# Attention probabilities turned by VectorE and DMA instead of TensorE, in a two-layer kernel in float32

## The chip, the cores and the metric

One core of a Trainium2 chip (trn2) runs the whole program. The metric is the device time of one execution in microseconds (us). Three runs of the kernel before took 1148.38, 1147.91 and 1146.68 us; the median is 1147.91 us. The profile is of one execution.

The engines are named as in the profile: PE is TensorE (PEld its weight loads), DVE is VectorE, ACT is ScalarE, POOL is GpSimd, SP is SyncE, whose queue issues nearly all DMAs here. SBUF and PSUM have 128 partitions; a "quarter" is 32 partitions that lie together.

## The reference, cut to what matters

The input x is 16 sequences of 256 tokens with 256 features, all in float32. Layer 0 is a normalisation, a linear recurrence and a gated feed-forward; the change does not touch it. Layer 1 is, with `S = 256`:

```
xn = layernorm(x)
q  = xn @ Wq                     # 16 heads, 128 plain + 64 rotary features
c, k_rope = split(xn @ Wkv_a)    # 64 latent + 64 rotary features, shared by all heads
k_nope, v = split(rmsnorm(c) @ Wkv_b)
scores = q . [k_nope, k_rope] / sqrt(192), masked so that a query sees keys up to itself
attn   = softmax(scores)
s      = (attn . v) @ Wo
x      = x + s * silu(base(x) + gated low-rank experts)
```

The kernel folds `Wkv_b` into the queries and into `Wo`. Each head then has queries of 128 features (64 latent, 64 rotary), all heads have the same keys `kT` (128 features) and the same 64 values per key (`row[:, :, 0:64]`), and attention returns 64 numbers per head and query.

## The kernel before

**Chunks and units.** The 4096 tokens are 8 chunks (`NCH`) of 512 (`CH`): two sequences, four blocks of 128 tokens. In layer 1 a chunk has 4 groups of 4 heads; a group has two units, one for each sequence (`b` = 0 and 1). So there are 64 units, 8 to a chunk, in the order chunk, group, sequence. A pair is the two units of one group.

**Scores of a unit** (`score_pack`, L644 to L675). The partitions hold 4 heads x 32 queries, so 8 query blocks `a` of 32 cover the sequence, and block `a` needs 32(a+1) keys. The blocks go in three packs, (7, 6), (5, 4, 3) and (2, 1, 0). For each pack PE writes `sc`, DVE adds the diagonal mask (L660) and takes the negative maximum `nm` (L662), ACT writes the exponentials to `pr` with their sum `sr` (L667), DVE inverts the sum (L672) and POOL scales `pr` (L675). Three `pr` buffers (`NPR = 3`) serve the units in turn.

**Turning the probabilities** (`turn_part`, L680 to L688). The value matmul needs keys on the partitions. For each unit PE transposes twelve 128x128 blocks of `pr` into the one buffer `pt` of PSUM, four blocks to a call, and ACT copies each 128x512 result to `pT`. The three calls of a unit stand in step i+2 of unit i (`LAG = 2`).

**Values of a unit** (`values`, L690 to L707): 8 matmuls of `pT` with `row` into `av`, then a DVE copy to `attT`. They stand in step i+3.

**Queries of the next group** (`query_tile`, L588 to L629), four tiles to a group, two in each step. Tiles 0 and 1 are the rotary part: DVE multiplies by the rotation (L610), POOL combines into `qrot` (L622, L623), and eight DMAs on SP's queue (L626) move quarters of `qrot` into partitions 64 to 127 of `qg`. Tiles 2 and 3 are the latent part, scaled by ACT into partitions 0 to 63 of `qg` (L616). Both go by PE (L606).

**Extras.** In each step one or two pieces of other work follow the packs: the preparation of the next chunk (`norm_chunk`, `transpose_chunk`, `kv_chunk`, `router_chunk`, `key_chunk`, `mid_chunk`, `gate_part`) and the output projection of the last one (`finish_part`, L709 to L721: 8 matmuls, a product on DVE, a sum on POOL, a DMA to HBM).

**Order.** The tile scheduler orders each engine's instructions from the program order and its own estimates. An engine then works its list strictly in that order. SP's queue, too, takes one DMA after the other, and a DMA whose data are not ready holds up those behind it.

Of the kernel before, what the change touches and what calls it, by code (L numbers as in the profile page):

```python
# [18 lines left out]
P = 128  # L19
B, S, D = 16, 256, 256  # L20
NTOK = B * S
CH = 512
# [17 lines left out]
@with_exitstack  # L40
def tile_two_layers(ctx: ExitStack, tc: tile.TileContext, d: dict, out: bass.AP):
    nc = tc.nc

    const = ctx.enter_context(tc.tile_pool(name="const", bufs=1))
    xpool = ctx.enter_context(tc.tile_pool(name="xres", bufs=1))
# [364 lines left out]
    pp = ctx.enter_context(tc.tile_pool(name="p1", bufs=2))  # L410
    fix = ctx.enter_context(tc.tile_pool(name="fix1", bufs=1))
    ps_sc = ctx.enter_context(tc.tile_pool(name="ps_sc", bufs=3, space=PSUM))
    ps_pt = ctx.enter_context(tc.tile_pool(name="ps_pt", bufs=1, space=PSUM))
    ps_m1 = ctx.enter_context(tc.tile_pool(name="ps_m1", bufs=4, space=PSUM))

    class Chunk:
        pass
# [14 lines left out]
    def kv_chunk(ch):  # L432

        k = chunks[ch]
        pkv = ps_m1.tile([P, TPC, P], F32, tag="m1", name=f"pkv_{ch}")
        for j in range(TPC):
            for c in range(2):
                nc.tensor.matmul(  # L438
                    pkv[:, j, :], k.xnT[:, c, j * P : (j + 1) * P], wkva[:, c, :],
                    start=(c == 0), stop=(c == 1),  # L440
                )
# [12 lines left out]
        ra = a2.tile([P, TPC, ROPE], F32, tag="ra", name=f"ra_{ch}", bufs=1)  # L454
        rb = a2.tile([P, TPC, ROPE], F32, tag="rb", name=f"rb_{ch}", bufs=1)
        nc.vector.tensor_tensor(ra[:, :, 0:HR], x1, rope_k[:, 0], ALU.mult)
        nc.vector.tensor_tensor(ra[:, :, HR:ROPE], x2, rope_k[:, 0], ALU.mult)
        nc.vector.tensor_tensor(rb[:, :, 0:HR], x2, rope_k[:, 1], ALU.mult)
        nc.vector.tensor_tensor(rb[:, :, HR:ROPE], x1, rope_k[:, 2], ALU.mult)
        nc.gpsimd.tensor_tensor(row[:, :, KVL:P], ra, rb, ALU.add)  # L460
        k.row = row

    def key_chunk(ch):
        k = chunks[ch]
        row = k.row
        pk = ps_m1.tile([P, CH], F32, tag="m1", name=f"pk_{ch}")
        for j in range(TPC):
            nc.tensor.transpose(pk[:, j * P : (j + 1) * P], row[:, j, :], ident)
        k.kT = a2.tile([P, CH], F32, tag="kT", name=f"kT_{ch}")
        nc.vector.tensor_copy(k.kT, pk)  # L470

    def router_chunk(ch):
# [4 lines left out]
        for jp in range(2):  # L477
            pm = ps_m1.tile([P, 2, 256], F32, tag="m1", name=f"pm_{ch}_{jp}")
            for j2 in range(2):
                j = 2 * jp + j2  # L480
                for c in range(2):
                    nc.tensor.matmul(  # L482
                        pm[:, j2, 0 : P + NE], k.xnT[:, c, j * P : (j + 1) * P], wmid[:, c, :],
                        start=(c == 0), stop=(c == 1),
                    )
# [46 lines left out]
    def mid_chunk(ch):  # L532
        k = chunks[ch]
        mg = k.mg
        pmT = ps_m1.tile([P, CH], F32, tag="m1", name=f"pmT_{ch}")
        for j in range(TPC):
            nc.tensor.transpose(pmT[:, j * P : (j + 1) * P], mg[:, j, :], ident)
        k.mT = a2.tile([P, CH], F32, tag="mT", name=f"mT_{ch}")
        nc.vector.tensor_copy(k.mT, pmT)

    def gate_part(ch, jp):
# [5 lines left out]
        for j2 in range(2):  # L547
            cols = slice((2 * jp + j2) * P, (2 * jp + j2 + 1) * P)
            for c in range(2):
                nc.tensor.matmul(  # L550
                    pg[:, j2, :], k.xnT[:, c, cols], wbase[:, c, :],
                    start=(c == 0), stop=False,
                )
            nc.tensor.matmul(pg[:, j2, :], k.mT[:, cols], wlb, start=False, stop=True)  # L554
# [17 lines left out]
    for h in range(G):  # L572
# [14 lines left out]
    def query_tile(ch, g, t):  # L587
# [3 lines left out]
        if t == 0:  # L591
            q = groups[ch, g] = Group()
            q.qg = qp.tile([P, CH // 32, G, 32], F32, tag="qg", name=f"qg_{n}")
            q.rot = qp.tile([P, 2, CH], F32, tag="qrot", name=f"qrot_{n}")
            q.mul = [
                qp.tile([P, 2, CH], F32, tag="qmul", name=f"qmul_{n}_{r}", bufs=3) for r in range(2)
            ]
        q = groups[ch, g]
        ps = ps_m1.tile([P, CH], F32, tag="m1", name=f"pq_{n}_{t}")
        for c in range(2):  # L600
            if t < 2:
                w = wrope[:, c, g, t, :, :].rearrange("p h f -> p (h f)")
            else:
                h0 = g * G + 2 * (t - 2)
                w = wlat[:, c, h0 : h0 + 2, :]
            nc.tensor.matmul(ps, w, k.xnT[:, c, :], start=(c == 0), stop=(c == 1))  # L606
        if t < 2:
            ps2 = ps.rearrange("p (b s) -> p b s", b=2)
            for r in range(2):
# [21 lines left out]
    class Unit:  # L631


        def __init__(self, i):
# [5 lines left out]
            self.nm = sm.tile([P, NQ], F32, tag="nm", name=f"nm_{self.n}")  # L640
            self.sr = sm.tile([P, NQ], F32, tag="sr", name=f"sr_{self.n}")

    def score_pack(u, pi):
        k, b, pack = chunks[u.ch], u.b, PACK[pi]  # L644
        qg = groups[u.ch, u.g].qg
        sc = ps_sc.tile([P, CH], F32, tag="sc", name=f"sc_{u.n}_{pi}")
        for a, o in pack:
            nc.tensor.matmul(  # L648
                sc[:, o : o + 32 * (a + 1)], qg[:, b * NQ + a, :, :].rearrange("p h q -> p (h q)"),
                k.kT[:, b * S : b * S + 32 * (a + 1)], start=True, stop=True,  # L650
            )
# [23 lines left out]
            nc.gpsimd.tensor_scalar(v, v, u.sr[:, a : a + 1], 1.0, ALU.mult, ALU.mult)  # L675


    BLOCKS = [(a, 0) for a in range(NQ)] + [(a, 1) for a in range(4, NQ)]

    def turn_part(u, z):  # L680
        if z == 2:
            u.pT = pp.tile([P, 12, P], F32, tag="pT", name=f"pT_{u.n}")
        pt = ps_pt.tile([P, CH], F32, tag="pt", name=f"pt_{u.n}_{z}")
        for y in range(4):
            a, kb = BLOCKS[4 * z + y]
            o = OFF[a] + kb * P
            nc.tensor.transpose(pt[:, y * P : (y + 1) * P], u.pr[:, o : o + P], ident)  # L687
        nc.scalar.copy(u.pT[:, 4 * z : 4 * z + 4, :], pt.rearrange("p (y f) -> p y f", y=4))  # L688

    def values(u):  # L690
        k, b = chunks[u.ch], u.b
        av = ps_m1.tile([P, 2, S], F32, tag="m1", name=f"av_{u.n}")
        for p2 in range(2):
            for kb in range(2):
                for hh in range(2):
                    hc = slice(32 * (2 * p2 + hh), 32 * (2 * p2 + hh) + 32)
                    nc.tensor.matmul(  # L697
                        av[64 * hh : 64 * hh + 64, p2, P * kb : S].rearrange(
                            "p (a q) -> p a q", q=32
                        ),  # L700
                        k.row[:, 2 * b + kb, 0:KVL],
                        u.pT[:, 8:12, hc] if kb else u.pT[:, 0:8, hc],
                        start=(kb == 0), stop=(kb == 1),
                    )
        if b == 0:
# [3 lines left out]
    def finish_part(ch, j):  # L709
        k = chunks[ch]  # L710
        po = ps_m1.tile([P, CH], F32, tag="m1", name=f"po_{ch}_{j}")
        for p in range(NPAIR):
            nc.tensor.matmul(  # L713
                po[:, 0:D], k.attT[p // 2][:, p % 2, j * P : (j + 1) * P], wout[:, p, :],
                start=(p == 0), stop=(p == NPAIR - 1),
            )
# [13 lines left out]
    router_chunk(0)  # L730
    key_chunk(0)
    mid_chunk(0)
    for jp in range(2):
        gate_part(0, jp)


    PER = 2 * NG
    LAG = 2
    LAST = NCH * PER
    units = {}  # L740
    turned = None
    for i in range(LAST + LAG + 1):
        ch, r = divmod(i, PER)

        extra = []
        if ch > 0 and LAG < r < LAG + 5:
            extra.append(lambda: finish_part(ch - 1, r - LAG - 1))
        if ch + 1 < NCH:
            extra += {
                0: [lambda: norm_chunk(ch + 1)],  # L750
# [5 lines left out]
                6: [lambda: gate_part(ch + 1, 0)],  # L756
                7: [lambda: gate_part(ch + 1, 1)],
            }[r]
        u = w = nq = None
        v = turned  # L760
        if i < LAST:
            u = units[i] = Unit(i)
            nxt = i // 2 + 1
            if nxt < LAST // 2:
                nq = (*divmod(nxt, NG), 2 * (i % 2))
        if LAG <= i < LAST + LAG:
            w = units.pop(i - LAG)
        extra += [None] * (2 - len(extra))
        for z in range(3):
            if u:  # L770
                score_pack(u, z)
            if v and z == 0:
                values(v)
            if w:
                turn_part(w, 2 - z)
            if z < 2:
                if nq:
                    query_tile(nq[0], nq[1], nq[2] + z)
                if extra[z]:
                    extra[z]()  # L780
        turned = w
    for j in range(TPC):
        finish_part(NCH - 1, j)


# [73 lines left out]
```

## Time and profile before

The profiled execution took 1148.42 us; its span from first to last instruction is 1146.3 us, so 2.1 us lie around the span.

| what | value |
|---|---|
| PE busy | 1052.2 us, 92% of the span |
| DVE busy | 518.2 us, 45% |
| ACT busy | 505.8 us, 44% |
| POOL busy | 403.0 us, 35% |
| granted TensorE clock, mean | 0.988 |
| layer 1: first and last score matmul start | 356.5 and 1106.8 us |
| one chunk in the steady part | 99.1 us (532.7 to 631.8) |
| PE transposes of `pr` (L687) | 768, 0.27 us each, 123.8 us busy |
| ACT copies to `pT` (L688) | 192, 0.59 us each, 112.9 us busy |
| DMAs of `qrot` to `qg` (L626) | 256, issue 0.585 to 1.9 us, median 0.627; landed 2.2 us after the issue began |

Busy time is the union of an engine's instructions. Matmuls are pipelined, so 0.27 us is how long one is under way; the next can start after about 0.12 us. A DMA's duration on SP is the issue only; its data land later.

### The profile page before, as it was taken

The page shows a single profiled execution, that of the slowest core. Times are in us where ns is not written, and L with a number is a line of the kernel's source. Part 1 is how long each engine was busy: PE and PEld are TensorE (multiplying, and loading weights), DVE is VectorE, ACT ScalarE, POOL GpSimd, SP SyncE. Part 2 cuts the span into 40 slices and gives each one's busy share as a digit, 9 for nine tenths or more (in the row PEclk, how much of TensorE's full clock was granted, in tenths as well). Part 3 has the DMA queues.
Part 4 walks back from the last instruction along what each step waited for, and adds up shares of the span by engine and source line. Part 5 has one row for each costly group of instructions (what it writes and reads, how often), then busy time and mean ns, then how long its engine had stood idle before and what let it go on. Part 6 is the DMA issues. An engine that isn't in the chain of part 4 may idle for free.

```text
span 1146.3 us, 16655 instructions
## 1 busy us (share of the span) xinstructions
PE 1052.2 (92%) x5506; PEld 756.6 (66%) x5506; DVE 518.2 (45%) x1841; ACT 505.8 (44%) x1520; POOL 403.0 (35%) x718
## 2 busy tenths in 40 slices
PE   1999999999968998999999899999999999999987
PEld 1567765666636665776677577667767767776765
DVE  5822222122176744644554454555455444545431
ACT  1232222322224566546545644654554465455450
POOL 3133223232243443333533343443334344334431
PEclk9999999999988999999999999999999999999998
DMA  9401000000011121111121111121111112111110
GB/s 312 151 2 44 2 0 1 1 1 1 0 19 19 19 37 21 24 28 24 28 37 29 21 23 33 22 35 34 24 20 28 29 27 35 28 24 26 30 21 19
DMA packets 154213, 36.60 MB, mean 32 GB/s; under 512 B 137232, under 2 KB 153616, under 8 KB 154128
## 3 DMA queue, kind: packets, MB, share of 16 engines
q1 hardware_dynamic: 151680, 32.78, 14.2%
q10 hardware_dynamic: 2448, 2.76, 0.7%
q8 instruction: 44, 0.72, 0.3%
q14 instruction: 41, 0.34, 0.1%
HBM read 14.55 MB, written 4.19 MB: 16 GB/s over the span
## 4 chain that ended last, share of the span: by engine, by line
PE 79%; ACT 8%; DVE 6%; issue 3%; DMA 2%; POOL 1%; SPq 0%; POOLq 0%; ACTq 0%; DVEq 0%
PE pq L606 17%; PE sc L648 11%; PE pf L393 9%; PE ph L353 9%; PE po L713 8%; PE av L697 8%; PE pt L687 7%; ACT pr L667 3%; PE pg L550 3%; ACT qg L616 2%; ACT pT L688 2%; PE py L391 1%; PE pg L554 1%; PE pm L482 1%; PE pkv L438 1%
## 5 line engine op out<-in xcount | busy, mean ns | idle before, releaser
L675 POOL TENSOR_SCALAR pr<-pr,sr 128x256 f32<-128x256 f32 (+7 forms) x512 | 189.4, 389 | 289.7 <-DVE sr L672 220.7
L667 ACT ACTIVATE pr<-sc,nm 128x256 f32<-128x256 f32 (+7 forms) x512 | 189.0, 380 | 74.7 <-DVE nm L662 66.6
L688 ACT COPY pT<-pt 128x512 f32<-128x512 f32 x192 | 112.9, 588 | 241.6 <-PE pt L687 241.2
L648 PEld LDWEIGHTS sc<-kT,qg 128*128 128x128 f32 x1024 | 157.8, 191 | 37.3 <-issue 22.9
L648 PE MATMUL sc<-kT,qg 128*128 128x256 f32 (+7 forms) x1024 | 173.8, 303 | 3.7 <-ACT qg L616 2.9
L687 PE MATMUL pt<-ident,pr 128*128 128x128 f32 x768 | 123.8, 281 | 14.5 <-ACT pT L688 14.5
L662 DVE TENSOR_REDUCE nm<-sc 128x1 f32<-128x256 f32 (+7 forms) x512 | 128.0, 300 | 3.8
L697 PE MATMUL av<-pT,row 128*64 128x256 f32 (+1 forms) x1024 | 101.7, 342 | 27.2 <-ACT pT L688 27.2
L606 PE MATMUL pq<-xnT,wrope 128*128 128x512 f32 x256 | 122.2, 601 | 0.2 <-ACT xnT L139 0.2
L606 PE MATMUL pq<-xnT,wlat 128*128 128x512 f32 x256 | 120.7, 593 | 0.0
L393 PE MATMUL pf<-p2T,hT 128*128 128x256 f32 x512 | 117.4, 380 | 0.0
L713 PE MATMUL po<-wout,attT 128*128 128x256 f32 x512 | 115.6, 379 | 0.0
L353 PE MATMUL ph<-xnT,p1T 128*128 128x512 f32 x256 | 113.6, 601 | 1.7 <-ACT xnT L139 1.7
L713 PEld LDWEIGHTS po<-wout,attT 128*128 128x128 f32 x512 | 97.3, 190 | 24.9 <-issue 11.8
L687 PEld LDWEIGHTS pt<-ident,pr 128*128 128x128 f32 x768 | 90.0, 147 | 29.2 <-issue 23.1
L610 DVE TENSOR_TENSOR qmul<-pq,rot_q 128x512 f32<-128x512 f32 x128 | 84.1, 682 | 54.0 <-PE pq L606 53.9
L393 PEld LDWEIGHTS pf<-p2T,hT 128*128 128x128 f32 x512 | 96.9, 190 | 16.3 <-issue 3.5
L697 PEld LDWEIGHTS av<-pT,row 128*64 128x64 f32 x1024 | 65.6, 140 | 63.0 <-ACT pT L688 40.9
L667 ACT ACTIVATION_READ_ACCUMULATOR pr<-sc,nm 128x1 f32 x512 | 104.0, 203 | 0.0
L353 PEld LDWEIGHTS ph<-xnT,p1T 128*128 128x128 f32 x256 | 48.4, 192 | 62.2 <-issue 53.9
L616 ACT ACTIVATE qg<-pq 64x512 f32<-64x512 f32 x128 | 75.8, 592 | 30.1 <-PE pq L606 28.2
L623 POOL TENSOR_TENSOR qrot<-qmul,qmul 128x512 f32<-128x512 f32 x32 | 40.8, 1274 | 94.4 <-DVE sr L672 55.1
(174 smaller groups left out, 1073.5 us busy)
## 6 DMA issues: line engine op xcount, KB each, us to landing
qg<-qrot SPq DMA_DIRECT2D x256, 64.0 KB, 2.2
x<-in_x_dram SPq DMA_DIRECT2D x8, 512.0 KB, 9.6
out_dram<-o SPq DMA_DIRECT2D x32, 128.0 KB, 1.7
wqn<-in_wq_nopeT_dram SPq DMA_DIRECT2D x4, 512.0 KB, 4.2
wo<-in_Wo_dram SPq DMA_DIRECT2D x4, 512.0 KB, 5.3
p1T<-in_proj1T_dram ACTq DMA_DIRECT2D x1, 1024.0 KB, 8.0
p2T<-in_proj2T_dram ACTq DMA_DIRECT2D x1, 1024.0 KB, 13.5
wraw<-in_wq_rope_dram SPq DMA_DIRECT2D x1, 1024.0 KB, 12.2
```

The source lines that it names most:

```text
L353: nc.tensor.matmul(ph, p1T[:, c, fc * P : (fc + 1) * P], xnT[:, c, :], start=(c == 0), stop=(c == 1),)
L393: nc.tensor.matmul(pf[:, j2, :], hT[fc][:, cols], p2T[:, fc, :], start=(fc == 0), stop=(fc == NFC - 1),)
L606: nc.tensor.matmul(ps, w, k.xnT[:, c, :], start=(c == 0), stop=(c == 1))
L616: nc.scalar.mul(q.qg[0:64, :, 2 * (t - 2) + hh, :], ps[64 * hh : 64 * hh + 64, :].rearrange("p (a q) -> p a q", q=32), SCALE,)
L648: nc.tensor.matmul(sc[:, o : o + 32 * (a + 1)], qg[:, b * NQ + a, :, :].rearrange("p h q -> p (h q)"), k.kT[:, b * S : b * S + 32 * (a + 1 ...
L662: nc.vector.tensor_reduce(u.nm[:, a : a + 1], sc[:, o : o + 32 * (a + 1)], AX.X, ALU.max, negate=True)
L667: nc.scalar.activation(u.pr[:, OFF[a] : OFF[a] + w], sc[:, o : o + w], AF.Exp, bias=u.nm[:, a : a + 1], accum_out=u.sr[:, a : a + 1],)
L675: nc.gpsimd.tensor_scalar(v, v, u.sr[:, a : a + 1], 1.0, ALU.mult, ALU.mult)
L687: nc.tensor.transpose(pt[:, y * P : (y + 1) * P], u.pr[:, o : o + P], ident)
L688: nc.scalar.copy(u.pT[:, 4 * z : 4 * z + 4, :], pt.rearrange("p (y f) -> p y f", y=4))
L697: nc.tensor.matmul(av[64 * hh : 64 * hh + 64, p2, P * kb : S].rearrange("p (a q) -> p a q", q=32), k.row[:, 2 * b + kb, 0:KVL], u.pT[:, 8: ...
L713: nc.tensor.matmul(po[:, 0:D], k.attT[p // 2][:, p % 2, j * P : (j + 1) * P], wout[:, p, :], start=(p == 0), stop=(p == NPAIR - 1),)
```

## The change

`turn_part` and the PSUM pool `ps_pt` go; `ps_m1` grows from 4 buffers to 5. In their place `turn(u)` makes three DVE transposes of 128x512, which turn every 32x32 block within its quarter, from `pr` into a new tile `t`. Then sixteen DMAs on SP's queue move quarter `h` of `t` (a head), columns `kb` (a block of 32 keys), to quarter `kb` of `pT`: 32 partitions x 3 runs of 128 float32, 48 KB each. Unit i-1 is turned in step i. The value matmuls of both units of a pair stand together in the odd steps (units i-3 and i-2 in step i), read `pT` in runs of 128, and are otherwise the same.

All layer-1 matmuls except the transposes of `xn` go through `InOrder`, which keeps TensorE's instructions in program order. `gate_part(ch, 1)` moves to the first step of its own chunk and `finish_part` to steps 2, 4, 5 and 6 of the next. Buffers change to make room: `pr` 3 to 2, `qrot` 2 to 1, `qmul` 3 to 2, `mT` 2 to 1; `pT` 2 to 3, `t` 2.

```diff
+    class InOrder:
+        def __init__(self, engine):
+            self.engine, self.last = engine, None
+        def __getattr__(self, name):
+            def call(*args, **kw):
+                r = getattr(self.engine, name)(*args, **kw)
+                if self.last is not None:
+                    tc.add_manual_dep(r.ins, self.last.name, ...)
+                self.last = r.ins
+                return r
+            return call
...
-    ps_pt = ctx.enter_context(tc.tile_pool(name="ps_pt", bufs=1, space=PSUM))
-    ps_m1 = ctx.enter_context(tc.tile_pool(name="ps_m1", bufs=4, space=PSUM))
+    ps_m1 = ctx.enter_context(tc.tile_pool(name="ps_m1", bufs=5, space=PSUM))
+    pe = InOrder(nc.tensor)
...
-    NPR = 3
+    NPR = 2
...
-    def turn_part(u, z):
-        if z == 2:
-            u.pT = pp.tile([P, 12, P], F32, tag="pT", name=f"pT_{u.n}")
-        pt = ps_pt.tile([P, CH], F32, tag="pt", name=f"pt_{u.n}_{z}")
-        for y in range(4):
-            a, kb = BLOCKS[4 * z + y]
-            o = OFF[a] + kb * P
-            nc.tensor.transpose(pt[:, y * P : (y + 1) * P], u.pr[:, o : o + P], ident)
-        nc.scalar.copy(u.pT[:, 4 * z : 4 * z + 4, :], pt.rearrange("p (y f) -> p y f", y=4))
+    THIRDS = ((0, 0), (4, 0), (4, 4))
+    def turn(u):
+        t = pp.tile([P, 3, 4, P], F32, tag="t", name=f"t_{u.n}")
+        u.pT = pp.tile([P, 3, G, P], F32, tag="pT", name=f"pT_{u.n}", bufs=3)
+        for z in (1, 2, 0):
+            a0, k0 = THIRDS[z]
+            o, w = OFF[a0], WID[a0]
+            nc.vector.transpose(
+                t[:, z, :, :].rearrange("p k (a q) -> p a k q", q=32),
+                u.pr[:, o : o + 4 * w].rearrange("p (a k s) -> p a k s", a=4, s=32)[
+                    :, :, k0 : k0 + 4, :
+                ],
+            )
+        for h in range(G):
+            for kb in range(4):
+                nc.sync.dma_start(
+                    u.pT[32 * kb : 32 * kb + 32, :, h, :], t[32 * h : 32 * h + 32, :, kb, :]
+                )
...
     def values(u):
...
-                        u.pT[:, 8:12, hc] if kb else u.pT[:, 0:8, hc],
+                    v = u.pT[:, 2:3, 2 * p2 + hh, :] if kb else u.pT[:, 0:2, 2 * p2 + hh, :]
...
         for z in range(3):
-            if u:
-                score_pack(u, z)
-            if v and z == 0:
-                values(v)
-            if w:
-                turn_part(w, 2 - z)
+            if i < LAST:
+                score_pack(units[i], z)
+            if z == 0 and i % 2 and i >= 3:
+                values(units[i - 3])
+                values(units[i - 2])
+            if z == 1 and 0 < i <= LAST:
+                turn(units[i - 1])
             if z < 2:
                 if nq:
                     query_tile(nq[0], nq[1], nq[2] + z)
                 if extra[z]:
                     extra[z]()
```

The line of `turn`'s DMAs is L719 in the changed kernel, of its DVE transposes L711.

More of the change, by code (lines that the diff above doesn't have):

```diff
@@ L42, in tile_two_layers @@
     nc = tc.nc
+    class InOrder:
[5 more added lines that the diff above has]
+                if self.last is not None:
+                    tc.add_manual_dep(
+                        r.ins, self.last.name,
+                        mybir.DependencyInfo(
+                            mybir.DependencyClass.NoSync, mybir.DependencyReason.DATA
+                        ),
+                        reason="order",
+                    )
+                self.last = r.ins
+                return r
+            return call
     const = ctx.enter_context(tc.tile_pool(name="const", bufs=1))
@@ L437, in kv_chunk @@
             for c in range(2):
-                nc.tensor.matmul(
+                pe.matmul(
                     pkv[:, j, :], k.xnT[:, c, j * P : (j + 1) * P], wkva[:, c, :],
@@ L467, in key_chunk @@
         for j in range(TPC):
-            nc.tensor.transpose(pk[:, j * P : (j + 1) * P], row[:, j, :], ident)
+            pe.transpose(pk[:, j * P : (j + 1) * P], row[:, j, :], ident)
         k.kT = a2.tile([P, CH], F32, tag="kT", name=f"kT_{ch}")
@@ L481, in router_chunk @@
                 for c in range(2):
-                    nc.tensor.matmul(
+                    pe.matmul(
                         pm[:, j2, 0 : P + NE], k.xnT[:, c, j * P : (j + 1) * P], wmid[:, c, :],
@@ L536, in mid_chunk @@
         for j in range(TPC):
-            nc.tensor.transpose(pmT[:, j * P : (j + 1) * P], mg[:, j, :], ident)
-        k.mT = a2.tile([P, CH], F32, tag="mT", name=f"mT_{ch}")
+            pe.transpose(pmT[:, j * P : (j + 1) * P], mg[:, j, :], ident)
+        k.mT = a2.tile([P, CH], F32, tag="mT", name=f"mT_{ch}", bufs=1)
         nc.vector.tensor_copy(k.mT, pmT)
@@ L549, in gate_part @@
             for c in range(2):
-                nc.tensor.matmul(
+                pe.matmul(
                     pg[:, j2, :], k.xnT[:, c, cols], wbase[:, c, :],
@@ L553, in gate_part @@
                 )
-            nc.tensor.matmul(pg[:, j2, :], k.mT[:, cols], wlb, start=False, stop=True)
+            pe.matmul(pg[:, j2, :], k.mT[:, cols], wlb, start=False, stop=True)
         nc.vector.tensor_tensor(k.g2[:, 2 * jp : 2 * jp + 2, :], pg, bc(bb_bc, 2), ALU.add)
@@ L593, in query_tile @@
             q.qg = qp.tile([P, CH // 32, G, 32], F32, tag="qg", name=f"qg_{n}")
-            q.rot = qp.tile([P, 2, CH], F32, tag="qrot", name=f"qrot_{n}")
+            q.rot = qp.tile([P, 2, CH], F32, tag="qrot", name=f"qrot_{n}", bufs=1)
             q.mul = [
-                qp.tile([P, 2, CH], F32, tag="qmul", name=f"qmul_{n}_{r}", bufs=3) for r in range(2)
+                qp.tile([P, 2, CH], F32, tag="qmul", name=f"qmul_{n}_{r}") for r in range(2)
             ]
@@ L605, in query_tile @@
                 w = wlat[:, c, h0 : h0 + 2, :]
-            nc.tensor.matmul(ps, w, k.xnT[:, c, :], start=(c == 0), stop=(c == 1))
+            pe.matmul(ps, w, k.xnT[:, c, :], start=(c == 0), stop=(c == 1))
         if t < 2:
@@ L639, in __init__ @@
             self.pr = prs[i % NPR]
-            self.nm = sm.tile([P, NQ], F32, tag="nm", name=f"nm_{self.n}")
-            self.sr = sm.tile([P, NQ], F32, tag="sr", name=f"sr_{self.n}")
     def score_pack(u, pi):
         k, b, pack = chunks[u.ch], u.b, PACK[pi]
+        if pi == 0:
+            u.nm = sm.tile([P, NQ], F32, tag="nm", name=f"nm_{u.n}")
+            u.sr = sm.tile([P, NQ], F32, tag="sr", name=f"sr_{u.n}")
         qg = groups[u.ch, u.g].qg
@@ L647, in score_pack @@
         for a, o in pack:
-            nc.tensor.matmul(
+            pe.matmul(
                 sc[:, o : o + 32 * (a + 1)], qg[:, b * NQ + a, :, :].rearrange("p h q -> p (h q)"),
@@ L675, in score_pack @@
             nc.gpsimd.tensor_scalar(v, v, u.sr[:, a : a + 1], 1.0, ALU.mult, ALU.mult)
-    BLOCKS = [(a, 0) for a in range(NQ)] + [(a, 1) for a in range(4, NQ)]
-    def turn_part(u, z):
-        if z == 2:
-            u.pT = pp.tile([P, 12, P], F32, tag="pT", name=f"pT_{u.n}")
-        pt = ps_pt.tile([P, CH], F32, tag="pt", name=f"pt_{u.n}_{z}")
-        for y in range(4):
-            a, kb = BLOCKS[4 * z + y]
-            o = OFF[a] + kb * P
-            nc.tensor.transpose(pt[:, y * P : (y + 1) * P], u.pr[:, o : o + P], ident)
-        nc.scalar.copy(u.pT[:, 4 * z : 4 * z + 4, :], pt.rearrange("p (y f) -> p y f", y=4))
+    THIRDS = ((0, 0), (4, 0), (4, 4))
[15 more added lines that the diff above has]
+                    u.pT[32 * kb : 32 * kb + 32, :, h, :], t[32 * h : 32 * h + 32, :, kb, :]
+                )
     def values(u):
@@ L695, in values @@
                 for hh in range(2):
-                    hc = slice(32 * (2 * p2 + hh), 32 * (2 * p2 + hh) + 32)
-                    nc.tensor.matmul(
+                    v = u.pT[:, 2:3, 2 * p2 + hh, :] if kb else u.pT[:, 0:2, 2 * p2 + hh, :]
+                    pe.matmul(
                         av[64 * hh : 64 * hh + 64, p2, P * kb : S].rearrange(
-                            "p (a q) -> p a q", q=32
+                            "p (z s) -> p z s", s=P
                         ),
-                        k.row[:, 2 * b + kb, 0:KVL],
-                        u.pT[:, 8:12, hc] if kb else u.pT[:, 0:8, hc],
+                        k.row[:, 2 * b + kb, 0:KVL], v,
                         start=(kb == 0), stop=(kb == 1),
@@ L712, in finish_part @@
         for p in range(NPAIR):
-            nc.tensor.matmul(
+            pe.matmul(
                 po[:, 0:D], k.attT[p // 2][:, p % 2, j * P : (j + 1) * P], wout[:, p, :],
@@ L732, in tile_two_layers @@
     mid_chunk(0)
-    for jp in range(2):
-        gate_part(0, jp)
+    gate_part(0, 0)
     PER = 2 * NG
-    LAG = 2
     LAST = NCH * PER
-    units = {}
-    turned = None
-    for i in range(LAST + LAG + 1):
+    FINISH = (2, 4, 5, 6)
+    units = [Unit(i) for i in range(LAST)]
+    for i in range(LAST + 3):
         ch, r = divmod(i, PER)
         extra = []
-        if ch > 0 and LAG < r < LAG + 5:
-            extra.append(lambda: finish_part(ch - 1, r - LAG - 1))
+        if r == 0 and ch < NCH:
+            extra.append(lambda: gate_part(ch, 1))
+        if ch > 0 and r in FINISH:
+            extra.append(lambda: finish_part(ch - 1, FINISH.index(r)))
         if ch + 1 < NCH:
@@ L755, in tile_two_layers @@
                 5: [lambda: mid_chunk(ch + 1)],
-                6: [lambda: gate_part(ch + 1, 0)],
-                7: [lambda: gate_part(ch + 1, 1)],
-            }[r]
[L759 to L767, printed above, removed]
+                6: [],
+                7: [lambda: gate_part(ch + 1, 0)],
+            }[r]
+        nq = None
+        nxt = i // 2 + 1
+        if nxt < LAST // 2:
+            nq = (*divmod(nxt, NG), 2 * (i % 2))
         extra += [None] * (2 - len(extra))
         for z in range(3):
-            if u:
-                score_pack(u, z)
-            if v and z == 0:
-                values(v)
-            if w:
-                turn_part(w, 2 - z)
+            if i < LAST:
[5 more added lines that the diff above has]
+                turn(units[i - 1])
             if z < 2:
@@ L780, in tile_two_layers @@
                     extra[z]()
-        turned = w
-    for j in range(TPC):
+    for j in range(1, TPC):
         finish_part(NCH - 1, j)
```

## The prediction

> **What bounds the kernel now.** I read the page's busy times first, then the granted clock, then the chain that ended last.
>
> ```profile
> PE 1052.2 (92%) x5506; PEld 756.6 (66%) x5506; DVE 518.2 (45%) x1841; ACT 505.8 (44%) x1520; POOL 403.0 (35%) x718
> ...
> PEclk9999999999988999999999999999999999999998
> ...
> PE 79%; ACT 8%; DVE 6%; issue 3%; DMA 2%; POOL 1%; SPq 0%; POOLq 0%; ACTq 0%; DVEq 0%
> ...
> L688 ACT COPY pT<-pt 128x512 f32<-128x512 f32 x192 | 112.9, 588 | 241.6 <-PE pt L687 241.2
> L687 PE MATMUL pt<-ident,pr 128*128 128x128 f32 x768 | 123.8, 281 | 14.5 <-ACT pT L688 14.5
> ```
>
> PE is the bound; the rest are half idle. So taking the transposes off PE pays at once, if nothing else becomes late. The windows of one chunk show the same: PE is busy in 93.83 of 99.10 us.
>
> ```profile
> 532.70:631.80 99.10, 93.83 (x553) 69.64 (x552) 51.24 (x187) 52.80 (x178) 39.15 (x79) 1.00 0.16 27
> ```
>
> The chain in order of time prices the transposes without their overlap (start, length, line, count):
>
> ```profile
> 604.59 0.59 PE sc L648 x6
> 605.18 0.48 PE pt L687 x4
> 605.67 0.02 issue
> 605.69 0.59 ACT pT L688
> ```
>
> Last, the queue that receives the new work. SP, in its source view and its timeline:
>
> ```profile
> L626 SPq DMA_DIRECT2D qg<-qrot x256: 585/627/1902, 333.7 to 1090.2; - x128
> ...
> 571.38 2.64 SPq L626 DMA_DIRECT2D qg<-qrot  x4
> ...
> L109 SPq DMA_DIRECT2D rot_q<-in_rope_q_dram x4: 414/420/582, 27.7 to 29.3; - x4
> ```
>
> Four `qg` moves take 2.64 us: one issue of 0.627 and three starts 0.67 us apart. That is 0.63 us of issue and 0.045 us between. The four loads of `rot_q` (32 partitions too, but from HBM) are the other end: 0.42 us, with the same gap 0.46.
>
> **What goes.** 768 PE transposes: four per 0.48 us in the chain, so 0.12 us each, 92 us in all or 2.9 us per pair. 192 ACT copies: 112.9 us busy, off the bound. A pair takes 99.10/4 = 24.8 us now, of which PE is busy 23.5; 20.6 stay.
>
> **What DVE gets.** 192 transposes of 128x512, which no row shows. The copy `attT` from PSUM of that size takes 0.69 us (L707); the slowest 128x512 product, from two SBUF inputs, 1.06 (L376). I take 0.69, for it has one input as the transpose has: 132 us, with 1.06 204 us. Per pair DVE goes from 51.24/4 = 12.8 to 16.9 us (19.2 at the upper end). It stays below 24.8 and costs nothing except latency: the last third of a unit, 0.7 us, lies behind POOL's scaling. Were DVE saturated, all of it would count.
> The Trainium skill (VectorE: DVE Perf Modes, Rules for kernel authors) speaks against the change: for a 128x128 transpose it says to use TensorE where the result may be in PSUM. Its table has 311 ns for VectorE at 128x128 in bf16; an estimate of four of those is 1.24 us for 128x512, or 20.3 us of DVE per pair. My sum is the same by both, since DVE stays under the pair; the trace prices TensorE's transpose at 0.12 us in the stream, where the page has 390 ns.
>
> **What SP gets.** 1024 DMAs, 32 per pair, in front of and behind the eight `qg` moves, in one list. In the built order it runs: 16 for one unit, 16 for the next (the output store between), then 8 for `qg`, and so on. Bounds for one new DMA, start to start: 0.46 us (the `rot_q` loads, 32 partitions, one run each) and 0.67 (the `qg` moves in a row). A price near zero is excluded: no issue on SP is under 0.32 us. I take 0.63: it is the only move from SBUF to SBUF between quarters in the trace, so `qg` is the nearest row, and its issue in an idle queue was 0.585, to which I add the gap of 0.045. I don't take the 0.67 because a `qg` move has 512 runs of 128 B and the new one 96 runs of 512 B.
> SP per pair: 32 x 0.63 = 20.2, eight `qg` moves 8 x 0.67 = 5.4, an output store 0.38: 26.0 us. That is above the 24.8 of today and far above PE's 20.6. SP becomes the bound.
> The Trainium skill (DMA: Bandwidth & Descriptors, Issuing engines are not separate DMA queues) says that the sequencer's time to initiate a DMA is usually small relative to the DMA itself. Here it isn't: eight `qg` moves hold SP for 5.4 us, and each lands 2.2 us after its start. By the rule the issue would drop out and the pair would be set by PE (the faster rival below); by the row it sets the time.
>
> **The time.** The first score is at 356.5 us and what precedes it is not changed. The first unit's DMAs can start once its scores, softmax and turn are done: step 0 takes about 10.7 us (half of the first pair's 21.4), and after the last score pack come 3.5 us to POOL's last scaling (619.82 + 0.75 to 624.03 in the timeline) and 0.7 us of DVE: 371. From there SP has 1024 x 0.63 = 645, 30 more `qg` groups 161, 28 stores 11: 817 us, to 1188. The last move lands 1.6 us later. Then values of the last unit 1.5, `attT` copy 0.7, four output projections 14.2 (64 matmuls at the end of the timeline) and 4.0 from there to the last store, as today: 1210 us of span. With 2.1 us around it 1212, and 0.5 less on the scale of the median (1147.91 against 1148.42): **1211 us**.
>
> **Waits and order.** TensorE in program order can't pass a value matmul whose `pT` is late, and behind it are the second and third score packs of the odd unit and the next queries. That closes a loop: values of a pair, then PE work up to the last score pack of the odd unit (value 1.5, two query tiles 3.4, two packs 1.4, extras 2.3: 8.6 us), softmax 3.5, turn 0.7, sixteen DMAs of which fifteen intervals and a landing of 2.2 count. It is 15.0 + 15 d per pair for a DMA interval d: 24.5 at 0.63, so SP's 26.0 ends last there. POOL writes `qrot` only when the previous group's eight moves have landed (one buffer); that is half a pair earlier in SP's list, so nothing is added, but if SP fell a whole pair behind, POOL's scalings behind `qrot` would wait too. `pr` with two buffers is freed by DVE one step before it is written. `qmul` and `mT` are read long before their next use. The value matmuls stay as many and as long (342 ns mean, pipelined).
>
> **Rivals.**
> *Issue is cheap* (faster): d = 0.46, as the later `rot_q` loads. SP then needs 20.5 us per pair, PE 20.6, the loop 21.9. 31 pairs x 21.9 = 679 against 750.6 from first to last score now; the tail (4.2 + 16 x 0.46 + 1.7 + 20.4 = 33.7 against 39.2) gives 5 more. 1146.3 - 72 - 5 = 1069, or 1071 with what lies around. For it: few, long runs. Against: it comes from loads, not moves. It decides from d under 0.57, where 371 + 1024 d + 172 + 22 equals the span of before.
> *Every move costs as `qg` in a row* (slower still): d = 0.67, 41 us more of SP: 1252. For it: it is what the nearest row shows at the very pattern, a burst.
> *Near balance*: d between 0.55 and 0.59: 1125 to 1170.
> *Clock* (slower): the slices show 8s where PE idled 3 to 6 us around 318 to 348 us. With SP as bound PE waits about 5 us per pair, and the clock can dip; PE has 5 us of slack for that, so I add nothing. In the faster rival the waits are about 1 us and the clock holds.
>
> **Chances.** Forecast 0.40, `qg` price in a row 0.18, cheap issue 0.32, near balance 0.10, split by sign. So slower 0.62, same 0.02, faster 0.36; about 0.2% (2.3 us) is what a measurement of this kernel can tell from no change. The range goes from 1070 to 1256, since the cheap issue alone holds a third; the forecast's own range is 1190 to 1256.
>
> **What would show it.** Right: L719's issues 0.58 to 0.63 us and SP without gaps; PE's longest waits at the value matmuls, ended by DMA into `pT`; 26 us per pair; PE busy down by about 90 us in a longer span. Wrong: L719 under 0.5 us, SP idle between turns. A DVE transpose over 1.5 us, or POOL waiting at `qrot`, would make it wrong in another way.

## The result: slower by 16%, and the profile after

The changed kernel takes 1331.58 us (median of 4 runs, 1330.64 to 1339.5) against 1148.14 us (1146.68 to 1148.47): a ratio of 1.162 with a 95% interval of 1.157 to 1.166. The direction was predicted, the size was not: 1331.6 lies 76 us above the upper end of the range. The profiled execution has a span of 1330.6 us at a mean granted clock of 0.904.

The page's busy times and clock slices after:

```profile
PE 1084.8 (82%) x4738; PEld 722.9 (54%) x4738; DVE 626.7 (47%) x2033; ACT 403.5 (30%) x1328; POOL 402.9 (30%) x717
...
PEclk9999999998878898888889888998898898888877
```

PE has 768 instructions fewer, yet it is busy 33 us longer, in a longer span. Before, the slices of layer 1 were nines; now most are eights. The groups tell where the busy time comes from (mean ns of one; idle before, and who ended it):

```profile
L52 PE MATMUL av<-pT,row 128*64 128x128 f32 (+1 forms) x1024 | 165.5, 380 | 154.0 <-DMA pT<-t 153.9
L52 PE MATMUL pq<-xnT,wlat 128*128 128x512 f32 x256 | 166.4, 786 | 0.0
L711 DVE STREAM_TRANSPOSE t<-pr 128x512 f32<-128x512 f32 x192 | 128.0, 694 | 56.3 <-POOL pr L699 52.7
```

The value matmuls wait 154 us for moves into `pT`, as predicted. Of the latent query matmuls that stand behind them, 98 of the 256 records took over 0.8 us (0.59 us before): these run at half clock, and the mean goes from 593 to 786 ns. The DVE transpose costs 0.694 us, as taken.

SP's new line, in its source view (duration min/median/max; landing likewise):

```profile
L719 SPq DMA_DIRECT2D pT<-t x1024: 585/597/1856, 371.3 to 1307.5; - x171
...
DMA to landing us min/median/max: 1.9/2.0/3.8
```

The first move starts at 371.3 us (371 predicted) and one issue costs 0.60 (median; 0.609 on average). But the last starts at 1307.5, not at 1188. The waits by engine show what is between:

```profile
SPq L753 <- POOL o L751: 80.1, 23, 9.5
...
SPq L719 <- DVE t L711: 12.4, 12, 1.5
```

SP stands idle 23 times, up to 9.5 us, before an output store (L753); 63.1 of these 80.1 us lie before the last move (worked out from the starts and lengths of SP's DMAs). One such place in SP's timeline (start, length, count):

```profile
770.14 8.28 SPq L719 DMA_DIRECT2D pT<-t  x13
778.58 5.92 SPq L649 DMA_DIRECT2D qg<-qrot  x8
789.99 0.34 SPq L753 DMA_DIRECT2D out_dram<-o  x1
```

From 784.50 to 789.99 SP does nothing, with sixteen moves of the next unit behind the store in its list. Their data were ready: DVE's last transpose of that unit ended at 777.5.

```profile
776.25 1.28 DVE L711 STREAM_TRANSPOSE t<-pr 128x512 f32<-128x512 f32 x2
```

The same stretch on PE:

```profile
777.80 0.62 PE L52 MATMUL av<-pT,row 128*64 128x256 f32 x2 [2.09 <-DMA pT<-t]
780.01 1.51 PE L52 MATMUL av<-pT,row 128*64 128x256 f32 x6 [1.59 <-DMA pT<-t]
781.45 3.78 PE L52 MATMUL pq<-xnT,wlat 128*128 128x512 f32 x4
785.03 3.66 PE L52 MATMUL po<-wout,attT 128*128 128x256 f32 x16
...
789.35 1.88 PE L52 MATMUL pq<-xnT,wlat 128*128 128x512 f32 x4
```

PE waits for SP's moves, then does the matmuls of one query tile (four records) at half clock (3.78 us where a tile takes 1.88 at 789.35), then the output projection `po` that the store is made of. So SP waits for PE, which had waited for SP. The chunk that holds this stretch takes 122.9 us, at a clock of 0.88 (the three beside it 118.9 to 119.7; before 99.1 us, PE 93.83). The chain that ended last breaks off 4% before the end of this run and is not read here. The window of the chunk:

```profile
703.60:826.50 122.90, 99.15 (x456) 66.19 (x456) 64.39 (x205) 39.93 (x153) 38.32 (x79) 0.88 0.39 74
```

### The profile page after: what moved, and what is told of

The parts are those of the page before. It is cut to its first block, busy times and chain, and to the rows that moved or that the text cites. A ratio compares the mean times of both kernels' runs of the same rounds, so it can differ in the third digit from the quotient of the medians.

```text
span 1330.6 us, 16812 instructions
## 1 busy us (share of the span) xinstructions
PE 1084.8 (82%) x4738; PEld 722.9 (54%) x4738; DVE 626.7 (47%) x2033; ACT 403.5 (30%) x1328; POOL 402.9 (30%) x717
## 5 line engine op out<-in xcount | busy, mean ns | idle before, releaser
L52 PE MATMUL av<-pT,row 128*64 128x128 f32 (+1 forms) x1024 | 165.5, 380 | 154.0 <-DMA pT<-t 153.9
L52 PEld LDWEIGHTS av<-pT,row 128*64 128x64 f32 x1024 | 85.5, 153 | 230.7 <-issue 135.7
L52 PEld LDWEIGHTS sc<-kT,qg 128*128 128x128 f32 x1024 | 155.1, 192 | 74.4 <-ACT qg L639 43.0
L52 PE MATMUL pq<-xnT,wlat 128*128 128x512 f32 x256 | 166.4, 786 | 0.0
L711 DVE STREAM_TRANSPOSE t<-pr 128x512 f32<-128x512 f32 x192 | 128.0, 694 | 56.3 <-POOL pr L699 52.7
L739 DVE COPY attT<-av 128x512 f32<-128x512 f32 x64 | 44.1, 689 | 145.2 <-PE av L52 144.5
L52 PEld LDWEIGHTS pq<-xnT,wlat 128*128 128x128 f32 x256 | 56.7, 245 | 55.5 <-issue 55.1
L52 PEld LDWEIGHTS pq<-xnT,wrope 128*128 128x128 f32 x256 | 48.0, 198 | 33.7 <-issue 32.5
```

Source lines behind the costliest of these rows:

```text
L52: r = getattr(self.engine, name)(*args, **kw)
L711: nc.vector.transpose(t[:, z, :, :].rearrange("p k (a q) -> p a k q", q=32), u.pr[:, o : o + 4 * w].rearrange("p (a k s) -> p a k s", a=4, ...
L739: nc.vector.tensor_copy(k.attT[u.g][:, :, b * S : (b + 1) * S], av)
```

## The experiments

The theory after the first reading: SP's list is the bound, through the number of issues, and on top of it the output store in that list closes a circle. In program order PE reaches `po` only after the value matmuls, these need the moves, and the next moves stand behind the store of `po`. The rivals: the values' own loop (values, softmax, turn, moves, values), the clock by itself, the bytes or the landings, and the program order by itself. All runs were timed beside the kernel before, which took 1147.6 to 1147.8 us in each group.

### Stores on another queue

```diff
-        nc.sync.dma_start(out_dram[t0 : t0 + P, :], o)
+        nc.gpsimd.dma_start(out_dram[t0 : t0 + P, :], o)
```

> The output stores go to GpSimd's queue; everything else is the changed kernel. Store theory: in the changed kernel SP stood idle for 63 us just before output stores, which wait for an output projection on TensorE; without them in SP's list the moves start at once and most of that comes back: 1265 to 1285 us. Loop theory (the ring from the value matmuls over scores, softmax, turn and sixteen moves, lengthened by the half clock, sets the pair): SP is idle elsewhere instead, 1315 to 1332 us.

Measured: 1260.51 us (1257.47 to 1262.13), ratio 1.098 [1.096, 1.100], 4.5 us below the store theory's bracket. The span is 72 us shorter. SP has no wait for a store among its waits; the one at its moves is for DVE's turn:

```profile
SPq L719 <- DVE t L711: 16.4, 16, 2.2
```

The window of one chunk, now 108.9 us, and the shares of the chain that ended last, where SP was 0% before the change:

```profile
789.49:898.42 108.93, 92.45 (x456) 63.41 (x456) 63.91 (x205) 39.90 (x153) 40.63 (x83) 0.94 0.44 83
```
```profile
PE 39%; SPq 34%; DVE 11%; POOL 5%; DMA 5%; issue 4%; ACT 2%; POOLq 0%; ACTq 0%; DVEq 0%
```

One line changed in one place, and 71 of the 183 us are gone: that the store's place in SP's list cost them is shown.

### Half of the moves on ACT's queue

```diff
-                nc.sync.dma_start(
+                (nc.sync if kb % 2 else nc.scalar).dma_start(
```

> Half of the sixteen moves of a unit (kb 0 and 2) go to ScalarE's queue. Issue theory: SP needs 16 x 0.64 + 5.4 + 0.4 = 16 us per pair instead of 26.5, and the ring shrinks by eight intervals (5 us), so a pair falls from 29.9 to 22 to 25 us: 1085 to 1180 us, unless ScalarE, which now waits for VectorE's turn in its list, holds back the exponentials. Landing theory (the time that a move needs to land sets it, not the issue): 1310 us or more.

Measured: 1193.71 us (1191.84 to 1194.99), ratio 1.040 [1.038, 1.042], 14 us above the issue theory's bracket. 138 us are gone, so SP's list was what bounded the changed kernel; each issue kept its price on both queues at once (median 0.597 us on SP, 0.610 on ACT). But ACT gives much back, as the expectation had feared: its exponentials stand behind moves in its own list (ACT's waits):

```profile
ACT pr L691 <- DMA pT<-t: 201.6, 43, 6.5
```

### Dummy matmuls where PE waits

```diff
+    def filler(i):
+        f = ps_m1.tile([P, CH], F32, tag="m1", name=f"f_{i}")
+        for z in range(FILL):
+            pe.matmul(f, ident, X[0].rearrange("p j e -> p (j e)")[:, 0:CH], start=True, stop=True)
+        nc.vector.tensor_copy(junk, f[:, 0:1])
+
+    FILL = 4
...
             if z == 0 and i % 2 and i >= 3:
+                filler(i)
                 values(units[i - 3])
                 values(units[i - 2])
```

> Adds four matmuls of 128x512 (0.86 us each at full clock, about 3.4 us per pair) on constant data in front of the value matmuls of each pair, and one 128x1 VectorE copy that is not used. Clock theory: TensorE waits there for 5 us anyway, so the filler is free, the clock stays up after the wait, and 1.7 to 5 us per pair come back: 1190 to 1290 us. SP theory: SP sets the time whatever TensorE's clock, so 1325 to 1345 us. Slower than 1350 us would mean that TensorE's own work is the bound.

Measured: 1295.68 us (1293.48 to 1299.09), ratio 1.129 [1.127, 1.132]: adding matmuls makes the kernel 36 us faster. It lies 6 us above the clock theory's bracket and 29 below the other's. The clock rose from 0.904 to 0.962, and SP's waits before the store fell from 80.1 to 48.5 us:

```profile
SPq L753 <- POOL o L751: 48.5, 17, 9.4
```

### Values two steps later

`pT` gets 4 buffers and `row` 3, `attT` and `o` lose one each, and `finish_part` stands in steps 4, 5, 6 and 6.

```diff
-            if z == 0 and i % 2 and i >= 3:
-                values(units[i - 3])
-                values(units[i - 2])
+            if z == 0 and i % 2 and i >= 5:
+                values(units[i - 5])
+                values(units[i - 4])
```

> The value matmuls of a pair come two steps later (units i-5 and i-4 in step i), with four buffers for the turned probabilities, three for row, five for attT, one for the output tile, and the output projections in steps 4 to 6. TensorE then has two steps of other work before it needs a moved tile. Ring theory: the ring is opened, SP alone sets the time, 26.5 us per pair without gaps: 1225 to 1260 us. If SP's list with its waits sets it: 1290 to 1330 us. If only the moves' landing mattered: under 1150 us.

Measured: 1260.48 us (1259.22 to 1261.93), ratio 1.099 [1.097, 1.101], the time of the stores on another queue to 0.1 us. PE reaches `po` without waiting for fresh moves, and the store's wait in SP's list is gone by itself (what is left lies almost all behind the last move):

```profile
SPq L753 <- POOL o L751: 18.2, 5, 8.9
```

The circle can be cut at either link with the same result. What remains between the first and the last move is nearly all issue on SP: of 865 us here SP was idle for 16, and of 862 with the stores moved for 28, mostly before moves. The low clock remains too (0.909 here, 0.922 with the stores moved).

### Stores moved and dummy matmuls together

> The kernel after with both edits: output stores on GpSimd's queue, and four dummy matmuls of 128x512 before the values of each pair. Theory (the clock costs only through the store that waits in SP's list): the store is out of the list, SP issues without gaps, so the filler changes nothing: 1250 to 1266 us, as with the stores alone, though the granted clock rises to 0.95 or more. Rival (the clock costs by itself): another 30 us go, 1215 to 1235 us.

Measured: 1253.75 us (1248.96 to 1254.58), ratio 1.092 [1.089, 1.095]. The clock is 0.966, and only 7 us come of it, where the same filler brought 36 with the store in SP's list. So the low clock cost mainly through the wait of the store.

### The program order alone, and the changed kernel without it

The first has only `InOrder` added to the kernel before, for its layer-1 matmuls and its transposes of `pr`; the second is the changed kernel without it:

```diff
-    pe = InOrder(nc.tensor)
+    pe = nc.tensor
```

> The kernel before with only TensorE's program order of layer 1 added; the turn by TensorE stays. Theory (the program order costs nothing where no transfer is late): 1140 to 1165 us. Rival (the order itself costs a good part of the 184 us): 1180 to 1300 us, with waits at the transposes of pr or at the values for ACT's copies.

> The kernel after with TensorE's order left to the scheduler instead of the program order. Theory (SP's list bounds, in whatever order PE works, and the store in it waits for PE's output projection): 1300 to 1350 us. Rival (program order makes PE wait where other work was ready): 1150 to 1260 us.

Measured: 1150.79 us (1149.64 to 1153.38), ratio 1.003 [1.002, 1.004], for the first; 1257.72 us (1254.56 to 1258.99), ratio 1.097 [1.095, 1.099], for the second. The expectation for the second was wrong, and the time lies near the rival's upper end: I had thought the store would wait in any order. SP's timeline without program order shows none of it; the store goes out between two moves:

```profile
759.82 4.14 SPq L719 DMA_DIRECT2D pT<-t  x6
764.06 0.53 SPq L753 DMA_DIRECT2D out_dram<-o  x1
764.70 10.62 SPq L719 DMA_DIRECT2D pT<-t  x16
775.42 5.30 SPq L649 DMA_DIRECT2D qg<-qrot  x8
```

So program order costs 3 us where no move is late, and 74 where the moves are: it is the third link of the circle. Three different cuts (the store's queue, the values' place, PE's order) end within 3 us of each other, with SP idle for 15 to 28 us in all between its first and last move.

### Moves of a third of the size

```diff
+        nc.vector.tensor_copy(u.pT[:, 1:3], t[:, 1:3])
...
-                    u.pT[32 * kb : 32 * kb + 32, :, h, :], t[32 * h : 32 * h + 32, :, kb, :]
+                    u.pT[32 * kb : 32 * kb + 32, 0:1, h, :], t[32 * h : 32 * h + 32, 0:1, kb, :]
```

with the stores on GpSimd's queue. This kernel leaves out the turn between quarters for two thirds of `pT`; it serves for its time alone.

> The kernel after with the output stores on GpSimd's queue, and each of the 1024 moves cut to a third: 32 partitions with one run of 512 bytes instead of three. The other two thirds of pT are copied by DVE within their partitions, not moved, so they are not turned between quarters. Theory (the price is for the DMA as such, 0.58 to 0.64 us whatever it carries): 1235 to 1270 us. Rival (the price goes with the runs, and one run costs as the loads of rot_q, 0.46 us start to start): SP has 1024 x 0.18 = 184 us less, and then PE or the loop bounds: 1090 to 1130 us.

Measured: 1263.36 us (1261.45 to 1266.82), ratio 1.102 [1.099, 1.104]: no gain against 1260.51. The source view of its moves:

```profile
L720 SPq DMA_DIRECT2D pT<-t x1024: 507/589/1677, 371.8 to 1240.3; - x171
```

A third of the bytes and of the runs, and the median issue goes from 0.597 to 0.589 us. Start to start, without waits, a move takes 0.643 us on average instead of 0.651 with the stores moved. These 8 us over 1024 moves go to longer waits for DVE (36.5 us before moves instead of 22.3), which has the copy to do as well. So neither the bytes nor the runs set the price.

### Fewer, larger DMAs through HBM

Four DMAs write the quarters of `t` to a scratch in HBM, ordered so that one DMA reads the unit's `pT` back: 5 issues for a unit in place of 16, with the bytes travelling twice. The two middle dimensions of `t` and of `pT` change places for it. The stores are on GpSimd's queue in these three kernels.

```diff
+        trip = dram.tile([4, 32, G, 3 * P], F32, tag="trip", name=f"trip_{u.n}")
         for h in range(G):
-            for kb in range(4):
-                nc.sync.dma_start(
-                    u.pT[32 * kb : 32 * kb + 32, :, h, :], t[32 * h : 32 * h + 32, :, kb, :]
-                )
+            nc.sync.dma_start(
+                trip[:, :, h, :].rearrange("k s f -> s k f"),
+                t[32 * h : 32 * h + 32, :, :, :].rearrange("p k z q -> p k (z q)"),
+            )
+        nc.sync.dma_start(
+            u.pT.rearrange("p h z q -> p (h z q)"), trip.rearrange("k s h f -> (k s) (h f)")
+        )
```

> The kernel after with the output stores on GpSimd's queue, and the sixteen moves of a unit replaced by five DMAs: four write quarters of t to a scratch in HBM, one reads it back into pT. The same bytes travel twice. SP then holds 2 x 5 moves at about 0.63 us, 6.3 us a pair instead of 20.2. Theory (the number of issues on SP sets the time): SP has about 12 us of issue a pair and is no bound; what is left is PE's 20.6 us or the loop, 12.8 us + 4 x 0.63 + two landings of 2.2 to 3.5 us, 20 to 22 us a pair: 1060 to 1110 us. Rival (the moved bytes or the landing, not the issue, set the time): twice the bytes and two landings in a row, 1180 us or more, and PE waits at the value matmuls for the read with SP idle.

Measured: 1359.3 us (1358.12 to 1359.99), ratio 1.185 [1.183, 1.187]. The rival was right on this kernel: PE waits for the read, with SP idle (the largest line of PE's waits for data, then of SP's):

```profile
PE av L52 <- DMA pT<-trip: 225.0, 49, 12.7
```
```profile
SPq L720 <- DVE t L712: 405.7, 35, 16.0
```

The writes took 3.8 us to land and the read 5.4. Whether bytes or latency, the next run tells: the same DMAs with the values two steps later, edited as above.

> As the kernel with the scratch in HBM, with the value matmuls two steps later (pT 4 buffers, row 3, attT 5, o 1), so that both landings have a pair's time to come in. Theory (issue count): PE is the bound again at 20.6 us a pair, 1050 to 1085 us, granted clock 0.97 or more, and faster than the kernel before. Rival (bytes): no gain against the kernel with the scratch alone, 1150 us or more.

Measured: 1139.28 us (1136.65 to 1139.54), ratio 0.993 [0.991, 0.994]. The same bytes, and 220 us less: latency in the values' loop, not bandwidth. This is 0.7% faster than the kernel before, but short of the forecast. The theory for that: the read waits in SP's list for its own writes, and the `qg` moves behind it wait too. The last kernel issues the read one step later:

```diff
         for z in range(3):
+            if z == 0 and 2 <= i <= LAST + 1:
+                read(units[i - 2])
             if i < LAST:
                 score_pack(units[i], z)
```

> As the kernel with the scratch in HBM and late values, with the read of a unit put one step later in SP's list, ahead of the writes of the next unit, so that the read no longer waits in the list for its own writes to land and the qg moves no longer wait behind it. Theory (what is left of the list is the wait of the read for its writes, some 5 us at the head of SP's list, which delays the qg moves): PE's waits before score matmuls fall from 81 to under 40 us and the time to 1075 to 1115 us. Rival (the transfers, not the list, are late; or PE's clock and order bound it): 1130 us or more.

Measured: 1100.65 us (1094.34 to 1103.82), ratio 0.959 [0.955, 0.962]: the fastest kernel of the study, 47 us ahead of the kernel before. The edit took 39 us. PE's waits before score matmuls fell from 81.5 to 57.6 us, less than expected, while the time came into the bracket. One chunk, and the clock slices:

```profile
793.49:882.92 89.43, 82.79 (x457) 60.10 (x457) 63.86 (x205) 39.64 (x153) 40.44 (x83) 1.00 0.66 171
```
```profile
PEclk9999999999997989999999999999999999999978
```

PE is busy 82.79 of 89.43 us at full clock: it is the bound again. That is 20.7 us of PE a pair, and 11.0 us less a chunk than before (93.83). The chunks before and after this one take 91.6 and 91.2 us, with PE busy for 84.5 at a clock of 0.98.

### Two queues, stores moved and values later together

> The kernel after with all three edits of the list: half of the moves on ACT's queue, output stores on GpSimd's, values two steps later. SP then has 16 x 0.64 + 5.4 = 15.7 us a pair, ACT 10.3 us of issue beside 11 us of work. Theory (issue is what bounds, and with it halved and nobody waiting for a landing PE bounds at 20.6 us): 1090 to 1150 us, granted clock over 0.96. Rival (ACT is held up in its list by moves whose t is not ready, as with two queues alone): 1175 to 1200 us, and the values two steps later change nothing.

Measured: 1200.47 us (1197.19 to 1208.64), ratio 1.047 [1.043, 1.052]; no better than the two queues alone (1193.71), as the rival had it. ACT's list is what holds:

```profile
ACT pr L691 <- DMA pT<-t: 184.9, 43, 7.1
```

One such wait in the timelines of DVE and ACT:

```profile
787.20 0.71 DVE L711 STREAM_TRANSPOSE t<-pr 128x512 f32<-128x512 f32 x1 [1.03 <-POOL pr L699]
...
787.94 2.55 ACTq L719 DMA_DIRECT2D pT<-t  x4
790.59 0.47 ACT L691 ACTIVATE pr<-sc,nm 128x256 f32<-128x256 f32 x1 [4.63 <-DMA pT<-t]
```

The rival's reason holds for the smaller part only. Of the 4.63 us that the exponential waits, 2.0 pass before the turn is done and 2.6 with four issues. The same goes for all gaps in ACT's work that end with an exponential right behind a move: of 212 us, 145 are issues and 53 waits for the first move's data (worked out from the starts and lengths of ACT's instructions). The sum of the theory counted ACT's issues as work beside its other work, not as a delay of the exponentials behind them. The later values can help with neither part, for both lie ahead of anything that PE does with the moved data.

## Why the prediction was wrong, step by step

**What goes: right.** 92 us of PE were to go, 2.9 us a pair, with 20.6 left. In the kernel where PE is free to run, 20.7 us are left and 2.8 went in the chunks at full clock (21.1 and 2.3 in the others). In the changed kernel itself the gain is hidden by PE's waits and its half clock.

**What DVE gets: right.** 0.69 us was taken, 0.694 measured; DVE is busy 64.39/4 = 16.1 us a pair, against 16.9. It cost one thing that the sum left out: SP waited 18.5 us in all before moves, 15 of them before the first move of a unit, for the turn.

**The price of an issue: nearly right.** Without the waits the moves started 0.653 us apart on average, taken at 0.63; that is about halfway to the 0.67 of the slower rival. Over 1024 moves it makes 668 us instead of 645. In the same way the `qg` groups took 168 us instead of 161 and the stores 12 instead of 11. Together that is 849 us from first to last move, 32 over the 817 of the sum.

**The step that failed: SP without gaps.** The sum counted an output store as 0.38 us of issue and nothing else. But the store has a wait of its own, for POOL's `o`, so for `po`, so for all that stands ahead of it in PE's program order, the value matmuls among them. The prediction named what is queued behind late values on PE (score packs and queries), and left out `po` and the store, though its own order of SP's list has the store between two units. The profile before had the wait as the first row of SP's waits, where it cost nothing because SP had little else to do:

```profile
SPq L721 <- POOL o L719: 242.5, 32, 29.5
```

In the changed kernel SP idled 63.1 us before stores, 18.5 before moves and 5.6 before `qg`: 87 us. With the 32 of the price that is the whole miss on SP: 849 + 87 = 936 us from 371.3 to 1307.5. The tail of 23.1 us was forecast at 22.0. With the store off SP's list the span is 1258.2: 72 us of the miss are the store, and the remaining 48 are the price, the turns and a slightly longer tail. So slower was right for the reason given, SP's issues, and not by luck; but three of the signs named in advance did not come: SP without gaps, 26 us a pair (about 30 measured), and PE busy for 90 us less (33 more).

**The clock: "I add nothing" was wrong, but by way of the same step.** PE was at half clock for 237 us of layer 1 (worked out from the clock records; 13 before). Where SP alone bounds, lifting the clock is worth 7 us, so PE's slack does cover most of it; where the store waits, it is worth 36 of its 72 us, since slow matmuls lie between the values and `po`.

**The loop.** The formula of 15.0 + 15d gave 24.5 us a pair, below SP's 26.0. Opening that loop gave the time that moving the store gives with the loop closed. SP's idle time before moves was 10.0 us against 22.3, while the 28 stores left in its list took 18. So the loop cost some 12 us at most and was not the bound, as argued.

**The rivals.** Cheap issue, at a third of the chance, rested on the loads of `rot_q` (0.46 us) and on their single run in each partition. The move cut to one run still starts every 0.64 us; the rest of the explanation, 96 long runs against 512 short ones, fails with it. That rival set the lower end of the range at 1070. The rule of the Trainium skill that stood for it (DMA: Bandwidth & Descriptors, Issuing engines are not separate DMA queues) doesn't hold for this list: it is held 0.60 us by each move that lands after 2.0, and 1024 of them make the bound.

**What stays open.** The kernel with the scratch and early values took 31 us a pair (124.5 us a chunk), where my estimate of the loop was 20 to 22; its parts were not taken apart.

## What to carry to other kernels

Before giving a queue a thousand small DMAs, multiply their number by the start-to-start time of the nearest like DMA, and then go through everything else in that queue for a wait of its own: a store at the head of the list holds up the moves behind it, and if the store's data depend on those moves' readers, the queue and the engine wait for each other. Fewer DMAs help where smaller ones do not, and latency that they add is hidden by consuming the data later and by issuing each dependent DMA when what it waits for has already landed. An engine's forced program order is nearly free (3 us here) only as long as nothing in it is late (74 us).

## What the runs showed of the hardware that I had not expected

The issue of a move between partition quarters hardly depends on what it carries: 0.597 us (median) for 48 KB in 96 runs of 512 bytes, 0.589 for 16 KB in 32. Those with one side in HBM were cheaper in the same SP list: 0.338 us for the reads of 768 KB and 0.43 for the writes of 192 KB, both medians in the fastest kernel, here by its source view (min/median/max). Which property sets it was not isolated.

```profile
L727 SPq DMA_DIRECT2D pT<-trip x64: 337/338/627, 377.5 to 1067.9; - x64
```
```profile
L719 SPq DMA_DIRECT2D trip<-t x256: 302/430/1342, 371.1 to 1062.1; - x128
```

The clock fell after short waits. The half clock of the stretch shown above began at 778.3 us, after a wait of 2.09 us, the first in PE's timeline for 17 us, and stayed for 6.8 us. The Trainium skill (TensorE: Matmul & The Clock Gate, Why this matters for your kernels) warns of idle gaps of more than about 3 us between bursts; here a gap of two thirds of that was followed by half clock. A wait of 1.64 us that ended at 760.52 was followed by 3.4 us of half clock from 761.2 on.
